# Group statistics without TensorE, the weighted sums' two halves as two tiles, and one running sum emitted later

## The chip, the core and the metric

The kernel runs on one core of a Trainium2 chip. The core has five engines that run at the same time and wait for one another through semaphores: TensorE (PE; its weight loads are shown apart, as PEld), VectorE (DVE), ScalarE (ACT), GpSimd (POOL) and SyncE (SP, which only issues DMAs here). The metric is the time of one execution in microseconds (us) of the device; the median of several runs counts, and less is better.

## What is computed

A batch of 16 images with 512 channels and 32 x 32 pixels goes through a group norm, attention over the 1024 pixels with four heads of 128 channels, and a projection, with the input added at the end. All is in 32-bit floats.

```python
xg = x.reshape(b, 8, -1)                      # 8 groups of 64 channels
mu, var = mean(xg), var(xg)
xn = ((xg - mu) * rsqrt(var + 1e-5)) * gamma + beta
q, k, v = split(qkv_w @ xn + qkv_b)           # per pixel, 3 x 512 channels
attn = softmax(q @ k.T * 128 ** -0.5)         # 4 heads, 1024 x 1024 each
out = proj_w @ (attn @ v) + proj_b
return x + out
```

## The kernel before

An image lies as four chunks of 128 channels (partitions) by 1024 pixels. The products with qkv_w and proj_w are done by Strassen's scheme in two levels (`two_levels`, `strassen`): 49 products of 128 x 128 by 256 pixels instead of 64, made by the matmuls of L604, with differences of the operands ahead of them (L572), evictions of the PSUM banks behind them (L484 and L626 on ACT, L628 on DVE) and sums of the results (L677). Its banks carry the tags x and y, two of each. The projection's last steps, L824 and L827, add bias and input on DVE and store the result.

The main loop goes through the attention steps `s`, 16 images x 4 heads x 8 blocks of 128 keys. A step works in two halves of 512 queries: `scores` makes the transposed scores of a block (L844) and their exponential on ACT (L850), `weighted_sum` of the block before adds up values by weights in PSUM (L912, the tile `po`), and at a head's last block ACT copies the result out (L919). The sum of the exponentials for the softmax is kept on DVE as a running sum `tot` over the blocks (L856, L858), and every image and head has `added[b, h, j]`, the instruction of block j's sum. Once per head `denominators` reduces `tot`, and `divide` (L922) applies the inverse.

Between these halves, the loop runs `units`: pieces of the neighbouring images' other work that `plan_head` lays into the head's eight blocks. Head 0 carries the second half of the image's q and k, head 1 the projection of the image before, head 2 the first half of the next image's q and k, head 3 the next image's v. Head 1 also has the next image's statistics: `load_x`, in blocks 2 and 3 `stats_chunk` for each chunk on ACT (two passes with an accumulator, L262 and L265, and copies that scale by 1/N, L263, L264, L268), then `stats_group`, then `normalise` (L109 on ACT, a few of image 1 on DVE by L112) in blocks 5 and 6, then the first differences of x (L317).

A group's 64 channels are half the partitions of a chunk, so the channels' means have to be averaged across partitions. `stats_group` does it by PE: a product of the 128 x 128 matrix `avg` (1/64 within each group) with the means, `pm` (L83), and one with the variances, `pv` (L88), each 4 columns wide. Around them stand small DVE instructions on 128 x 4 elements (L82, L84 to L87, L89), a power of -0.5 on POOL (L90), and scale and shift (L76, L100, L102). A product of 32-bit floats takes two PE instructions, so pm and pv are four.

The order in which an engine gets its instructions is made ahead of time by a planner. It goes by the order of emission, moves what stands under `tc.high_priority(URGENT)` ahead, takes into account when it reckons the operands to be ready, and keeps an instruction under `tc.issue_after(i)` behind `i` on that engine. Each engine then runs its instructions strictly in that order, and waits where an operand or a tile isn't free. A tile of a pool is free for its next use when all that read the last one are done.

Image 0 is a special case: its own statistics are done in an opening, and its first heads also prepare the weights' Strassen sums for v and the projection on DVE (`kept_group`, L424 to L439), store them in DRAM (L441), and load them back as needed (L406).

Of the kernel before, what the change touches and what calls it, by code (L numbers as in the profile page):

```python
# [10 lines left out]
F32 = mybir.dt.float32  # L11
I32 = mybir.dt.int32
AF = mybir.ActivationFunctionType
# [3 lines left out]
P = 128  # L17
# [169 lines left out]
def fast_path(ctx, tc, x, sources, out, consts, flag, dims):  # L187
# [33 lines left out]

    spans = one.tile([BLK, B * HEADS], F32, name="spans")
    ones = one.tile([BLK, 1], F32, name="ones")
    xs, xb, vs, qs, ks, os_, ob = {}, {}, {}, {}, {}, {}, {}
    mvs, scaled = {}, {}

# [19 lines left out]
    for g in range(P // GC):  # L246
        nc.vector.memset(avg[ts(g, GC), ts(g, GC)], 1.0 / GC)
    nc.vector.memset(neghalf, -0.5)
    for t, src in (
        (gamma_sb, gamma), (beta_sb, beta), (qkb_sb, qk_b), (vb_sb, v_b), (projb_sb, proj_b)  # L250
    ):
        nc.gpsimd.dma_start(t, src)
# [1 line left out]
    norm = Norm(nc, gn, ps_a, avg, neghalf, gamma_sb, beta_sb, NCC, N, "y")  # L254

    def stats_chunk(b, c):
        if c == 0:
            mvs[b] = gn.tile([P, NCC, 2], F32, tag="mv", name=f"mv_{b}")

        junk = lpool.tile([P, N], F32, tag="tt", name=f"junk_{b}_{c}")  # L260
        sums = gn.tile([P, 3], F32, tag="st", name=f"sums_{b}_{c}")
        nc.scalar.activation(junk, xs[b, c], AF.Identity, accum_out=sums[:, 0:1])  # L262
        nc.scalar.mul(mvs[b][:, c, 0:1], sums[:, 0:1], 1.0 / N)  # L263
        nc.scalar.mul(sums[:, 1:2], sums[:, 0:1], -1.0 / N)  # L264
        nc.scalar.activation(  # L265
            junk, xs[b, c], AF.Square, bias=sums[:, 1:2], accum_out=sums[:, 2:3]
        )
        nc.scalar.mul(mvs[b][:, c, 1:2], sums[:, 2:3], 1.0 / N)  # L268

    def stats_group(b):  # L270


        g = []

        def part(n, first, last):
            if not g:
                g.extend(norm.group_steps(mvs[b]))
            with tc.issue_after(added[b - 1, 1, n].ins), tc.high_priority(URGENT):
                for step in g[first:last]:
                    step()  # L280

        def scale():
            n = 4 if b > 1 else 3
            part(n, 9, 10)
            with tc.issue_after(added[b - 1, 1, n].ins), tc.high_priority(URGENT):
                mu, sc = norm.result
                sh = norm.shift(mu, sc)
            for c in range(NCC):
                scaled[b, c] = sc, sh, c

        return [lambda: part(2, 0, 6), lambda: part(3, 6, 9), scale]

    def normalise(b, c, half, on_scalar=True):
        t = xs[b, c][:, ts(half, HALF)]
# [171 lines left out]
    def run(units):  # L466
        for u in units:
            u()
# [372 lines left out]
    def scores(s, half):  # L841
        b, h, j = where(s)
        sc = ps_s.tile([P, HALF], F32, tag="s", name=f"s_{s}_{half}")
        nc.tensor.matmul(  # L844
            sc, ks[b, h][:, ts(j, P)], qs[b, h][:, ts(half, HALF)], start=True, stop=True
        )
        if half == 0:
            ps[s] = ppool.tile([P, N], F32, tag="p", name=f"p_{s}")
        with tc.high_priority(URGENT):
            exps[s] = nc.scalar.activation(ps[s][:, ts(half, HALF)], sc, AF.Exp, scale=SCALE)  # L850
        i = ts(half, HALF) if s == steps - 1 else ds(0, N)
        if j == 0 or (half == 0 and s < steps - 1):
            return
        if j == 1:
            tot[b, h] = lpool.tile([P, N], F32, tag="tot", name=f"tot_{b}_{h}")
            nc.vector.tensor_add(tot[b, h], ps[s - 1], ps[s])  # L856
        else:
            added[b, h, j] = nc.vector.tensor_add(  # L858
                tot[b, h][:, i], tot[b, h][:, i], ps[s][:, i]
            )  # L860
# [45 lines left out]

    def weighted_sum(s, half):
        b, h, j = where(s)
        if j == 0 and half == 0:
            po[b, h] = ps_o.tile([P, N], F32, tag="o", name=f"po_{b}_{h}")  # L910
        i = ts(half, HALF)
        nc.tensor.matmul(  # L912
            po[b, h][:, i], v_block(b, h, j), ps[s][:, i],
            start=(j == 0), stop=(j == NB - 1),
        )
        if j == NB - 1:
            if (b, h) not in os_:
                os_[b, h] = opool.tile([P, N], F32, tag="o", name=f"o_{b}_{h}")
            last_eviction[b] = nc.scalar.copy(os_[b, h][:, i], po[b, h][:, i])  # L919

    def divide(b, h):
        nc.vector.tensor_mul(os_[b, h], os_[b, h], rinv.pop((b, h)))  # L922
# [136 lines left out]
    def plan_head(b, h):  # L1059

        plan = [[] for _ in range(NB)]
        if h == 0:
            spread(plan, staggered(next_qk.pop()), 0, NB)
            if b > 0:
                plan[6].append(lambda: o_blocks(b - 1))
                plan[6].append(lambda: sums_of_b(ob[b - 1]))
            else:
                plan[5].append(lambda: stage_blocks("v"))
        elif h == 1:
            if b > 0:  # L1070
                spread(plan, staggered(proj_groups(b - 1)), 0, NB)
            if b + 1 == B:
                plan[0].append(lambda: last_loads("x"))
            else:
                plan[0].append(lambda: load_x(b + 1))
                spread(plan, [lambda c=c: stats_chunk(b + 1, c) for c in range(NCC)], 2, 4)
                sums, power, scale = stats_group(b + 1)
                if b == 0:

                    plan[4] += [sums, power, scale]  # L1080
                else:
                    plan[4].insert(0, sums)
                    plan[4].insert((len(plan[4]) + 1) // 2, power)
                    plan[5].insert(0, scale)
                for r in range(2):
                    plan[5 + r] += [

                        lambda c=c, half=half: normalise(b + 1, c, half, b > 0 or c % 2 == 1)
                        for c in range(KC * r, KC * r + KC) for half in range(NH2)
                    ]  # L1090
                plan[6].append(lambda: x_sums(b + 1, (1,)))
            if b == 0:
                for g in range(len(OUTER)):
                    plan[g // 2].append(lambda g=g: kept_group("v", g))
                    plan[NB // 2 - 1 + g].append(lambda g=g: kept_group("proj", g))
                plan[2].append(lambda: stage_blocks("proj"))
                spread(plan, [lambda o=o: bias_of_v(o) for o in range(NCC)], 3, 5)
        elif b + 1 == B:
            if h == 2:
                plan[0].append(lambda: last_loads("w"))  # L1100
                plan[2].append(last_bias)
            else:
                os_[b, h] = opool.tile([P, N], F32, tag="o", name=f"o_{b}_{h}")
                plan[3].append(lambda: o_blocks(b))
                plan[3].append(lambda: sums_of_b(ob[b], (1,)))
                plan[5].append(lambda: sums_of_b(ob[b], (2, 3), (0,)))
        elif h == 2:
            spread(plan, staggered(qk_groups(b + 1, 0)), 0, NB)

            plan[0].insert(2, lambda: x_sums(b + 1, (2,)))  # L1110
            plan[1].append(lambda: x_sums(b + 1, (3,)))
        else:

            spread(plan, staggered(next_v.pop()), 0, NB - 1)

            plan[NB - 2].append(lambda: ahead[f"qk_{b + 1}_1"]())
        return plan
# [93 lines left out]
    for s in range(steps + 1):  # L1211
        units = []
        if s < steps:
            b, h, j = where(s)
            if j == 0:
                plan = plan_head(b, h)
            units = plan[j]
            if j == NB - 1 and h == 2 and b + 1 < B:
                next_v.append(v_groups(b + 1))
                next_qk.append(qk_groups(b + 1, 1))  # L1220
                units.append(ahead[f"v_{b + 1}"])
        if NB < s < steps and s % NB == 1:
            denominators(*where(s - 2)[:2])
        for half in range(NH2):
            if s < steps:
                scores(s, half)
                if j in (1, 2) and half == 1 and s > NB:
                    with tc.issue_after(exps[s].ins):
                        spread_inverse(*where(s - NB)[:2], j - 1)
                if half == 1 and j == 4 and s > NB:  # L1230

                    with tc.issue_after(added[b, h, 4].ins):
                        divide(*where(s - NB)[:2])
            if s > 0:
                weighted_sum(s - 1, half)
            n = (len(units) + 1) // 2
            run(units[half * n : (half + 1) * n])
        if s > 0:
            del ps[s - 1]

# [135 lines left out]
```

## Time and profile before

| What | Value |
|---|---|
| median of 3 runs | 3169.19 us (3167.69 to 3172.65) |
| the profiled execution | 3171.08 us |
| its span from first to last instruction | 3169.3 us |
| granted TensorE clock | 1.0 of full speed |
| L912 and L844, weighted sums and scores on PE | 1049.4 and 1047.4 us busy |
| pm (L83) and pv (L88) on PE, 4 columns, 30 instructions each | 4.3 and 5.8 us busy |
| L858, running sums on DVE | 470.2 us busy |
| DMA | 165 GB/s over the span |

A row of the timeline has the start and the busy time in us, the engine, the line of the kernel, the operation with output and inputs, the shape, the number of instructions merged in the row, and in brackets the idle time ahead of it with what ended it. Instructions of one engine overlap in the records, since the next starts while the last one drains; the distance from start to start tells what an instruction holds its engine for. A row of the chain has start, duration, engine and line.

### The profile page before, as it was taken

To read this page: it belongs to the slowest core of one execution; us is meant where nothing else is said; L and a number is where in the kernel's file an instruction comes from. 1 tells how busy PE (TensorE), PEld (TensorE's weight loads), DVE (VectorE), ACT (ScalarE), POOL (GpSimd) and SP (SyncE) were. 2 spreads that over 40 slices of the span, in tenths; PEclk is the share of its full clock that TensorE was granted. 3 is DMA by queue.
4 is the path that set the end of the run, shared out by engine and by line. 5 is a ranking of instruction groups with operands and counts; after the bars stand their busy time and mean duration, and the time that the engine had idled before them with its cause. 6 is when DMAs were issued, how large, how long until landed. Compare 5 with 4: busy or idle time off the path is not lost.

```text
span 3169.3 us, 34227 instructions
## 1 busy us (share of the span) xinstructions
PE 3156.8 (100%) x10502; PEld 2188.2 (69%) x10502; DVE 2635.8 (83%) x4642; ACT 1438.3 (45%) x2711; POOL 516.3 (16%) x896
## 2 busy tenths in 40 slices
PE   9999999999999999999999999999999999999999
PEld 7566676677776776767767667677676776766664
DVE  9878879788897888878888787987879978788785
ACT  3535435354353443535435454453534545344333
POOL 0011221111211112211122111222012221122200
PEclk9999999999999999999999999999999999999999
DMA  5554554545545555454554545555455564555531
GB/s 176 186 190 154 187 173 152 173 152 194 168 164 163 155 184 176 167 165 144 193 173 159 170 144 192 167 174 171 144 177 170 176 187 133 178 158 187 180 119 48
DMA packets 210668, 524.83 MB, mean 166 GB/s; under 512 B 32176, under 2 KB 65456, under 8 KB 210480
## 3 DMA queue, kind: packets, MB, share of 16 engines
q1 hardware_dynamic: 133088, 282.39, 28.6%
q0 software_dynamic: 64000, 204.54, 19.3%
q10 hardware_dynamic: 13392, 35.66, 3.5%
q8 instruction: 86, 1.41, 0.2%
q14 instruction: 102, 0.84, 0.1%
HBM read 389.30 MB, written 133.17 MB: 165 GB/s over the span
## 4 chain that ended last, share of the span: by engine, by line
PE 96%; DVE 2%; DMA 1%; issue 0%; SPq 0%; POOL 0%; ACT 0%; ACTq 0%; DVEq 0%
PE s L844 27%; PE po L912 27%; PE qk_x L604 12%; PE qk_y L604 9%; PE pp_x L604 6%; PE v_x L604 6%; PE v_y L604 4%; PE pp_y L604 4%; PE lx L999 0%; DVE qk_t L572 0%; DMA x<-in_x 0%; PE ly L999 0%; DVE tot L858 0%; DVE qk_r L628 0%; DVE qk L712 0%
## 5 line engine op out<-in xcount | busy, mean ns | idle before, releaser
L912 PE MATMUL po<-p,v 128*128 128x512 f32 x2048 | 1049.4, 594 | 0.7 <-ACT p L850 0.7
L850 ACT ACTIVATE p<-s 128x512 f32<-128x512 f32 x1024 | 610.6, 596 | 963.7 <-PE s L844 960.0
L844 PE MATMUL s<-qk,qk 128*128 128x512 f32 x2048 | 1047.4, 593 | 0.3 <-DVE qk L712 0.3
L912 PEld LDWEIGHTS po<-p,v 128*128 128x128 f32 x2048 | 603.6, 302 | 322.7 <-issue 214.5
L858 DVE TENSOR_TENSOR tot<-tot,p 128x1024 f32<-128x1024 f32 x385 | 470.2, 1221 | 158.1 <-ACT p L850 156.1
L844 PEld LDWEIGHTS s<-qk,qk 128*128 128x128 f32 x2048 | 387.7, 190 | 88.6 <-issue 29.9
L604 PEld LDWEIGHTS qk_x<-qk_t,w 128*128 128x128 f32 x1344 | 251.8, 190 | 166.1 <-issue 75.3
L604 PE MATMUL qk_x<-qk_t,w 128*128 128x256 f32 x1344 | 356.3, 382 | 0.1
L484 ACT COPY qk_u<-qk_x 128x512 f32<-128x512 f32 (+1 forms) x256 | 136.2, 532 | 229.6 <-PE qk_x L604 229.6
L777 POOL DMA_DIRECT2D vd<-vu x120 | 66.6, 556 | 902.9 <-DVE vu L769 899.5
L628 DVE TENSOR_TENSOR qk_r<-qk_y,qk_u 128x512 f32<-128x512 f32 (+1 forms) x256 | 158.1, 618 | 34.7 <-ACT qk_u L484 21.5
L578 POOL DMA_DIRECT2D kept_t<-qk_t x240 | 129.3, 540 | 278.5 <-DVE qk_t L572 212.0
L604 PEld LDWEIGHTS pp_x<-pp_t,w_proj 128*128 128x128 f32 x630 | 117.2, 190 | 74.7 <-issue 32.3
L628 DVE TENSOR_TENSOR v_r<-v_y,v_u 128x512 f32<-128x512 f32 (+1 forms) x120 | 76.6, 638 | 110.5 <-ACT v_u L484 80.3
L604 PE MATMUL pp_x<-pp_t,w_proj 128*128 128x256 f32 x630 | 167.8, 383 | 0.0
L782 POOL DMA_DIRECT2D v<-vd x240 | 140.5, 592 | 166.6 <-DMA vd<-vu 63.3
L604 PE MATMUL v_x<-v_t,w_v 128*128 128x256 f32 x630 | 166.6, 381 | 0.0
L828 POOL DMA_DIRECT2D out_y<-y x120 | 65.9, 550 | 603.3 <-DVE y L827 601.5
L604 PEld LDWEIGHTS v_x<-v_t,w_v 128*128 128x128 f32 x630 | 118.4, 190 | 55.3 <-issue 19.1
L604 PE MATMUL qk_y<-x,w 128*128 128x256 f32 x512 | 142.2, 379 | 1.5 <-DVE qk_r L628 1.5
L769 DVE STREAM_TRANSPOSE vu<-vt 128x512 f32<-128x512 f32 x120 | 135.7, 1131 | 4.5 <-DMA vd<-vu 4.4
L712 DVE SCALAR_TENSOR_TENSOR qk<-qk_r,qkb_sb,qk_r 128x512 f32<-128x512 f32 x192 | 137.7, 744 | 1.6
(203 smaller groups left out, 4420.0 us busy)
## 6 DMA issues: line engine op xcount, KB each, us to landing
w<-kept SPq DMA_DIRECT2D x90, 512.0 KB, 3.7
kept_t<-qk_t POOLq DMA_DIRECT2D x180, 256.0 KB, 3.5
v_t<-kept_t SPq DMA_DIRECT2D x180, 256.0 KB, 2.9
w<-kept SPq DMA_DIRECT2D x90, 384.0 KB, 3.3
rinv<-row ACTq DMA_DIRECT2D x63, 512.0 KB, 5.0
x<-in_x POOLq DMA_DIRECT2D x60, 512.0 KB, 4.6
vd<-vu POOLq DMA_DIRECT2D x120, 256.0 KB, 3.0
v<-vd POOLq DMA_DIRECT2D x240, 128.0 KB, 4.2
```

Source lines behind the costliest of these rows:

```text
L484: nc.scalar.copy(t[n][:, :width], t["x"][:, :width])
L578: nc.gpsimd.dma_start(t, to)
L604: nc.tensor.matmul(acc[:, ts(i, Q)], have["w"][t][:, i, slot, :], inner(i, bn), start=(first and i == 0), stop=True, skip_group_check=True,)
L628: nc.vector.tensor_add(dst, view(a), view(c))
L712: nc.vector.scalar_tensor_tensor(st[b, h][:, ts(half, HALF)], a, qkb_sb[:, i : i + 1], c, ALU.add, ALU.add)
L769: nc.vector.transpose(u.rearrange("p (q i j) -> p j q i", q=n, i=BLK), t.rearrange("p (j q i) -> p j q i", q=n, i=BLK),)
L777: nc.gpsimd.dma_start(rows[which][ts(h, P), :], u)
L782: nc.gpsimd.dma_start(vs[b, pair][ts(q, BLK), half].rearrange("m h (k i) j -> m (h k) (i j)", k=n), rows[which].rearrange("(k m) (q e) -> ...
L844: nc.tensor.matmul(sc, ks[b, h][:, ts(j, P)], qs[b, h][:, ts(half, HALF)], start=True, stop=True)
L850: exps[s] = nc.scalar.activation(ps[s][:, ts(half, HALF)], sc, AF.Exp, scale=SCALE)
L858: added[b, h, j] = nc.vector.tensor_add(tot[b, h][:, i], tot[b, h][:, i], ps[s][:, i])
L912: nc.tensor.matmul(po[b, h][:, i], v_block(b, h, j), ps[s][:, i], start=(j == 0), stop=(j == NB - 1),)
```

## The change

There are three parts.

1. For images 1 to 15, the group statistics no longer use PE. ACT writes the means and the sums of squares of each chunk into columns of a tile `table` of 128 x 2 x 32, zero elsewhere, and one copy per chunk is gone. `gather` then works on DVE: it sets the counts, transposes the table in blocks of 32 x 32, so that a channel's numbers lie along a row, copies each half of a group to the other's partitions (four copies), aggregates 64 triples by one `bn_aggr`, adds epsilon, and has POOL raise one column to -0.5. `scale` transposes mean and inverse deviation back and makes scale and shift. `gather` comes behind block 3's running sum, `scale` behind block 4's (in image 0 both behind block 3's); before, there were three parts, behind blocks 2, 3 and 4.
2. The weighted sums' PSUM tile of two banks becomes two tiles of one bank, `o0` and `o1`, one for each half.
3. In head 1, block 6, of images 1 to 14, the running sum is emitted behind all other units of that block and not between its halves.

```diff
+    table = one.tile([P, 2, BLK], F32, name="table")
...
+    nc.gpsimd.memset(table, 0.0)
...
     def stats_chunk(b, c):
-        if c == 0:
-            mvs[b] = gn.tile([P, NCC, 2], F32, tag="mv", name=f"mv_{b}")
-
+        mean, spread_ = (
+            (mvs[b][:, c, 0:1], mvs[b][:, c, 1:2]) if b == 0
+            else (table[:, 0, c : c + 1], table[:, 1, c : c + 1])
+        )
...
-        nc.scalar.mul(mvs[b][:, c, 0:1], sums[:, 0:1], 1.0 / N)
+        nc.scalar.mul(mean, sums[:, 0:1], 1.0 / N)
...
-            junk, xs[b, c], AF.Square, bias=sums[:, 1:2], accum_out=sums[:, 2:3]
+            junk, xs[b, c], AF.Square, bias=sums[:, 1:2],
+            accum_out=sums[:, 2:3] if b == 0 else spread_,
         )
-        nc.scalar.mul(mvs[b][:, c, 1:2], sums[:, 2:3], 1.0 / N)
+        if b == 0:
+            nc.scalar.mul(spread_, sums[:, 2:3], 1.0 / N)
...
+        def gather():
+            t["all"] = lpool.tile([P, N], F32, tag="tt", name=f"groups_{b}")
+            rows = t["all"][:, : 6 * BLK].rearrange("p (s j) -> p s j", s=3)
+            both = t["both"] = t["all"][:, 6 * BLK : 6 * BLK + 2]
+            ve = t["all"][:, 6 * BLK + 2 : 6 * BLK + 3]
+            v.memset(rows[:, 0, :], float(N))
+            v.transpose(rows[:, 1:3, :BLK], table)
+            for q in range(quads):
+                v.tensor_copy(rows[ts(q, BLK), 1:3, BLK:], rows[ts(q ^ 1, BLK), 1:3, :BLK])
+            v.bn_aggr(both, rows.rearrange("p s j -> p j s"))
+            v.tensor_scalar_add(ve, both[:, 1:2], EPS)
+            nc.gpsimd.tensor_tensor(both[:, 1:2], ve, neghalf[:, 0:1], ALU.pow)
 
         def scale():
-            n = 4 if b > 1 else 3
-            part(n, 9, 10)
-            with tc.issue_after(added[b - 1, 1, n].ins), tc.high_priority(URGENT):
-                mu, sc = norm.result
-                sh = norm.shift(mu, sc)
+            back = t["all"][:, 8 * BLK : 10 * BLK].rearrange("p (s j) -> p s j", s=2)
+            v.transpose(back, t["both"].unsqueeze(2).to_broadcast([P, 2, BLK]))
+            sc = gn.tile([P, NCC], F32, tag="sc", name="sc")
+            v.tensor_mul(sc, back[:, 1, k], gamma_sb)
+            sh = norm.shift(back[:, 0, k], sc)
             for c in range(NCC):
                 scaled[b, c] = sc, sh, c
 
-        return [lambda: part(2, 0, 6), lambda: part(3, 6, 9), scale]
+        def part(n, step):
+            with tc.issue_after(added[b - 1, 1, n].ins), tc.high_priority(URGENT):
+                step()
+
+        return [lambda: part(3, gather), lambda: part(4 if b > 1 else 3, scale)]
...
             exps[s] = nc.scalar.activation(ps[s][:, ts(half, HALF)], sc, AF.Exp, scale=SCALE)
+        if not (h == 1 and j == 6 and 0 < b < B - 1):
+            running_sum(s, half)
+
+    def running_sum(s, half):
+        b, h, j = where(s)
         i = ts(half, HALF) if s == steps - 1 else ds(0, N)
...
-        if j == 0 and half == 0:
-            po[b, h] = ps_o.tile([P, N], F32, tag="o", name=f"po_{b}_{h}")
+        if j == 0:
+            po[half] = ps_o.tile([P, HALF], F32, tag=f"o{half}", name=f"po_{b}_{h}_{half}")
...
-                sums, power, scale = stats_group(b + 1)
+                gather, scale = stats_group(b + 1)
                 if b == 0:
-
-                    plan[4] += [sums, power, scale]
+                    plan[4] += [gather, scale]
                 else:
-                    plan[4].insert(0, sums)
-                    plan[4].insert((len(plan[4]) + 1) // 2, power)
+                    plan[4].insert(0, gather)
                     plan[5].insert(0, scale)
...
             run(units[half * n : (half + 1) * n])
+        if s < steps and h == 1 and j == 6 and 0 < b < B - 1:
+            running_sum(s, 1)
```

More of the change, by code (lines that the diff above doesn't have):

```diff
@@ L270, in stats_group @@
+        if b == 0:
+            nc.scalar.mul(spread_, sums[:, 2:3], 1.0 / N)
     def stats_group(b):
[L273 to L277, printed above, removed]
-            with tc.issue_after(added[b - 1, 1, n].ins), tc.high_priority(URGENT):
-                for step in g[first:last]:
-                    step()
-        def scale():
-            n = 4 if b > 1 else 3
-            part(n, 9, 10)
-            with tc.issue_after(added[b - 1, 1, n].ins), tc.high_priority(URGENT):
-                mu, sc = norm.result
-                sh = norm.shift(mu, sc)
+        v = nc.vector
@@ new lines, in stats_group @@
+        quads = P // BLK
+        k = slice(0, NCC)
+        t = {}
+        def gather():
[10 more added lines that the diff above has]
+            nc.gpsimd.tensor_tensor(both[:, 1:2], ve, neghalf[:, 0:1], ALU.pow)
@@ L908, in weighted_sum @@
         b, h, j = where(s)
-        if j == 0 and half == 0:
-            po[b, h] = ps_o.tile([P, N], F32, tag="o", name=f"po_{b}_{h}")
+        if j == 0:
+            po[half] = ps_o.tile([P, HALF], F32, tag=f"o{half}", name=f"po_{b}_{h}_{half}")
         i = ts(half, HALF)
         nc.tensor.matmul(
-            po[b, h][:, i], v_block(b, h, j), ps[s][:, i],
+            po[half], v_block(b, h, j), ps[s][:, i],
             start=(j == 0), stop=(j == NB - 1),
@@ L918, in weighted_sum @@
                 os_[b, h] = opool.tile([P, N], F32, tag="o", name=f"o_{b}_{h}")
-            last_eviction[b] = nc.scalar.copy(os_[b, h][:, i], po[b, h][:, i])
+            last_eviction[b] = nc.scalar.copy(os_[b, h][:, i], po[half])
     def divide(b, h):
```

## The prediction

> **What bounds the kernel now.** I read the page's busy times and its chain first, then the waits, then the timeline of one middle image on PE and on DVE, and at last the chain in image 0.
>
> ```profile
> PE 3156.8 (100%) x10502; PEld 2188.2 (69%) x10502; DVE 2635.8 (83%) x4642; ACT 1438.3 (45%) x2711; POOL 516.3 (16%) x896
> ...
> PE 96%; DVE 2%; DMA 1%; issue 0%; SPq 0%; POOL 0%; ACT 0%; ACTq 0%; DVEq 0%
> ```
>
> PE is busy all the time and carries 96% of the chain, and the list of waits names only 6 us in which PE waited. So PE's own instructions are the time, and an edit gains if it takes instructions or bubbles from PE's row, and loses if PE begins to wait. A busy share can hide bubbles, so I read starts instead. First the middle image's statistics in head 1 (columns: start, us, engine, line, what, count):
>
> ```profile
> 1094.26 1.03 PE L604 MATMUL pp_x<-pp_t,w_proj 128*128 128x256 f32 x4
> 1095.12 0.28 PE L83 MATMUL pm<-mean,avg 128*128 128x4 f32 x2
> 1095.26 1.11 PE L604 MATMUL pp_x<-ot,w_proj 128*128 128x256 f32 x4
> 1096.21 1.02 PE L844 MATMUL s<-qk,qk 128*128 128x512 f32 x2
> ...
> 1101.81 0.59 PE L604 MATMUL pp_y<-ot,w_proj 128*128 128x256 f32 x2
> 1102.33 0.39 PE L88 MATMUL pv<-vv,avg 128*128 128x4 f32 x2
> 1102.57 1.10 PE L844 MATMUL s<-qk,qk 128*128 128x512 f32 x2
> 1103.52 1.02 PE L912 MATMUL po<-p,v 128*128 128x512 f32 x2
> ```
>
> From start to start, four 256-column instructions take 0.86 us (1094.26 to 1095.12). Around the two averages the row stretches: pm itself holds 0.14 us (to 1095.26), and the next four instructions take 0.95 instead of 0.86; two pp_y ahead of pv take 0.52 instead of 0.43, pv holds 0.24, and the next two s take 0.95 instead of 0.86.
>
> **The change part by part.** *The averages leave PE.* pm costs 0.14 + 0.09 = 0.23 us, pv costs 0.09 + 0.24 + 0.09 = 0.42 us; with the unrounded starts 0.64 us per image. Images 2 to 15 lose both products: 14 x 0.64 = **8.9 us**, on the path. Nothing that PE does next is late: what follows pm and pv reads data that lay ready.
>
> The Trainium skill's page "TensorE: Matmul & The Clock Gate", section "Step-by-step: what each phase is for", speaks against this gain: weight loads are pulled ahead of running matmuls, so the next weights load while a matmul runs. By that rule the four small instructions would be nearly free; here the rows above measure 0.64 us, because a 4-column matmul is too short to cover the load behind it.
>
> *The averages of image 1* (made during image 0) sit elsewhere. PE waited 1.22 us there for the mean, but what PE gains in image 0 it gives back:
>
> ```profile
> 149.82 3.96 DMA kept_proj<-w_proj
> 153.79 5.28 DMA w<-kept
> ...
> 159.21 1.97 PE qk_x L604 x8
> ```
>
> PE stops for the weights that land 5.28 us after 153.79, and the chain behind that DMA is DVE's preparation of w_proj, which runs without idle time from 129.1 us but for 0.93 us ahead of sc (waiting for rstd). So here DVE sets the time, and its work grows. Removed: nine small instructions (mean to sh), each followed by the next 0.07 to 0.11 us after its start, 0.75 us in all, and the 0.93 us wait. Added, the gather: a 64-column memset and a 64-column transpose at 0.13 each (a DVE instruction here holds its engine for its recorded time less 0.08; L875 with 32 columns took 0.19, elementwise work adds 1.04 ns a column); four copies between groups of 32 partitions at 0.20 (L872 to L873, which also change partitions, start 0.19 to 0.20 apart); one bn_aggr over 192 numbers; one add at 0.07. bn_aggr's nearest row is L52, 12 numbers in 0.209 us, 0.059 above the 0.15 of the smallest instructions: at one number a cycle 192 cost 0.27, by that row's slope 0.94. Three results are read by the next instruction, 0.1 us each. That gives 1.8 to 2.5 us; I take 2.0, near the first slope since L49 (bn_stats, 512 columns, 0.69) runs at one column a cycle. The scale part: transpose 0.13, three small ones 0.21, three dependent steps 0.3: 0.65. The power on POOL, now one column, took 0.72 us for two columns, 1.08 for four at this place and 2.03 later on; I allow DVE a wait of 0.6, between 0 and 0.93. Sum for image 0: 2.0 + 0.65 + 0.6 - 0.75 - 0.93 = **1.6 us lost** (0.8 to 2.4). PE's own earlier time there goes into the wait for the weights.
>
> *The gather and scale in images 1 to 14.* They cost nothing if PE never waits for DVE. The cover is idle DVE time, and there is little of it:
>
> ```profile
> 1097.89 1.23 DVE L858 TENSOR_TENSOR tot<-tot,p 128x1024 f32<-128x1024 f32 x1 [0.61 <-ACT p L850]
> 1099.04 0.75 DVE L572 TENSOR_TENSOR pp_t<-ot,pp_t 128x256 f32<-128x256 f32 x2
> 1099.71 0.68 DVE L827 TENSOR_TENSOR y<-y,pp_r 128x512 f32<-128x512 f32 x1
> 1101.58 0.69 DVE L628 TENSOR_TENSOR pp_r<-pp_y,pp_p 128x512 f32<-128x512 f32 x1 [1.19 <-PE pp_y L604]
> ...
> 1120.23 0.42 DVE L628 TENSOR_TENSOR pp_r<-pp_y,pp_u 128x256 f32<-128x256 f32 x1
> ...
> 1121.17 1.22 DVE L858 TENSOR_TENSOR tot<-tot,p 128x1024 f32<-128x1024 f32 x1
> ```
>
> The gather comes behind the sum at 1097.89, so its inputs (ACT's last square ends at 1095.7) are there and it adds no wait. Between 1099 and 1103 DVE idles 1.5 us; of the gather's 2.0 some 0.5 stays over. From 1102.4 to 1131 the busy row shows 28.41 us of 28.60 for DVE: nothing absorbs there. The scale adds 0.65 less the 0.21 of sc, t and sh: 0.45. So DVE is about 0.9 us late after 1107 (0.6 to 1.5), against a PE that is 0.64 early. The power hides: the gather ends near 1101, the scale may not start before the sum at 1104.92 ends, and 2.03 us fit between. Behind the waiting power POOL queues the loads of y and the stores of out_y, which today wait at the same place for ve, at 1103.2, later than the gather ends. Behind the scale DVE queues o's division and the sums; it waits for nothing that is late. ACT loses one small copy per chunk and is 45% busy: nothing.
>
> Which PE wait is next? The last y bank of the projection: DVE ends reading it at 1120.65, PE writes it again at 1121.71, and its weights (0.19) load in between, so some 0.85 us are to spare. The first differences of the next image's q/k (done 1125.24, wanted at 1127.5) have 2.2 us. I take **no stall**, for one reason that the trace shows: DVE's order is not the order of emission. x's differences (L317, emitted last in block 6) run at 1113.11, ahead of that block's sum, and evictions (L628, marked urgent) stand between y's finishing steps (L824, L827), which no engine waits for soon. Eight finishing steps of 0.6 us lie from 1115.45 to 1121.17; added DVE work should push those back, not the evictions.
>
> *The running sum of block 6* moves behind its block's other work. In the trace it already runs at 1121.17, behind all but one eviction, so moving it gains nothing by itself. It guards the order above. Its readers are the sum at 1122.68 and, behind that, the differences with 2.2 us to spare; beyond that each us of lateness is one of PE.
>
> *Two tiles for the weighted sums.* In image 15, where no other products stand between heads, PE's second half waits for ACT's copy of the first half, and the next head for the second copy:
>
> ```profile
> 3082.80 1.02 PE L844 MATMUL s<-qk,qk 128*128 128x512 f32 x2
> 3083.66 1.23 PE L912 MATMUL po<-p,v 128*128 128x512 f32 x2
> ```
>
> The pair at 3083.66 lasts 0.21 us longer than its like; this occurs five times after 3080: **1.0 us** gained. In image 0 the same costs 0.08 four times, lost to the wait above. In the other images no such bubble shows. The memset of the table puts some tenths of a us ahead of POOL's first loads (gamma goes out at 1.3 us and is used at 10.5): nothing.
>
> **The sum.** -8.9 - 1.0 + 1.6 = -8.3 us. The profiled execution took 3171.08 us (span 3169.3, 1.8 around it), 1.9 above the median of 3169.19. It holds a PE wait of 1.49 us at 2998.9 behind one DMA of 5.4 us (median of its kind 3.0), which no other image has. So I put the sum on the median: **3160.9 us**. What a measurement here can tell from no change is about 0.2%, 6.3 us; the forecast is 0.26%.
>
> **The rivals.** *DVE's order stays and the y bank comes late.* Then 0.9 + 0.64 - 0.85 = 0.7 us of PE wait per image, 14 x 0.7 = 9.8: 3170.7 us, no change. For it: DVE without idle time from 1102 on. Against it: the finishing steps that can give way. *The same wait at its upper price, slower:* DVE 1.5 late gives 1.3 per image, 18 us: 3179. It decides from 1.04 us of wait per image, (8.3 + 6.3) / 14. Each 1.22 us sum that slips ahead of an eviction would do it too. *The small products were free anyway:* then only pm's and pv's matmul starts (28 ns apart) go, 14 x 4 x 0.028 = 1.6 us, and with +1.0 - 1.6 the time is 3168.2. The rows above speak against it. This is what the Trainium skill's rule above would give.
>
> **How the numbers follow.** The forecast (no stall, or under 0.15 us per image) has 0.57. The y bank late by 0.15 to 1.04 us has 0.24, free products 0.04: together 0.28 within 0.2%. Late by more, 0.15. The low end is 8.3 with image 0 at its lower bound and the lowest run as base: 3167.7 - 9.1 = 3158.6, less 1.6 if the DMA hiccup sits in the median too: 3157. The high end is the first rival, 3171; above it lies most of the slower case.
>
> **What would show it.** PE's count falls by 60; in head 1 four 256-column instructions keep 0.86 us throughout, and the same product of two images in a row is 195.1 us apart instead of 195.8 (pp_y's pieces of the chain at 695.92 and 891.69). Weights in image 0 land at about 160.7. DVE's row without idle reaches further, with evictions still ahead of L824 and L827. I am wrong if PE shows a bubble at pp_y's last product in head 1, or if the gather holds DVE over 2.5 us.

## The result and the profile after

| Kernel | Median of 10 runs each | Ratio, 95% interval | Its profiled execution |
|---|---|---|---|
| before | 3169.03 us (3167.6 to 3172.65) | | 3171.08 us, span 3169.3 |
| after | 3161.18 us (3159.85 to 3162.99) | 0.9975 [0.9967, 0.9984] | 3160.22 us, span 3158.5 |

The change gains 7.9 us, a quarter of a per cent (5 to 10 us by the interval); 3160.9 had been forecast. The page of the kernel after, busy times and chain:

```profile
PE 3147.1 (100%) x10442; PEld 2181.1 (69%) x10442; DVE 2655.5 (84%) x4687; ACT 1433.7 (45%) x2651; POOL 497.0 (16%) x897
...
PE 96%; DVE 2%; DMA 1%; issue 0%; SPq 0%; ACT 0%; POOL 0%; ACTq 0%; DVEq 0%; POOLq 0%
```

PE has 60 instructions less and is as much the bound as before; DVE has 19.7 us more work. The span shrank by 10.8 us, more than the medians differ, since before's profile holds a DMA hiccup. Read from the starts of the images' first scores (L844 before, L862 after): the 14 distances from image 1 on lost 8.1 us in sum, typically 195.22 instead of 195.79, or 0.57 each with the unrounded starts. Image 0 took 180.94 instead of 180.33, 0.6 more. In image 1 one more wait of before is gone, 0.24 us at a weighted sum (at 431.89). Image 15 lost 2.8: 1.0 for the bubbles and 1.65 for that hiccup. The rest, 0.1 and 0.4, lies ahead of image 0 and behind the last product.

The statistics of a middle image, on DVE, in the timeline of the kernel after:

```profile
1095.61 1.22 DVE L881 TENSOR_TENSOR tot<-tot,p 128x1024 f32<-128x1024 f32 x1 [0.83 <-ACT p L868]
1096.79 0.11 DVE L288 MEMSET groups<- 128x64 f32 x1
1096.82 0.19 DVE L289 STREAM_TRANSPOSE groups<-table 128x64 f32<-128x64 f32 x1
1096.93 0.38 DVE L590 TENSOR_TENSOR pp_t<-ot,pp_t 128x256 f32<-128x256 f32 x1
1097.33 0.78 DVE L291 COPY groups<-groups 32x64 f32<-32x64 f32 x4
1098.14 0.42 DVE L590 TENSOR_TENSOR pp_t<-ot,pp_t 128x256 f32<-128x256 f32 x1
1098.48 1.01 DVE L292 BATCH_NORM_AGGREGATE groups<-groups 128x2 f32<-128x192 f32 x1
1099.41 0.63 DVE L845 TENSOR_TENSOR y<-y,pp_r 128x512 f32<-128x512 f32 x1
1099.96 0.14 DVE L293 TENSOR_SCALAR groups<-groups 128x1 f32<-128x1 f32 x1
1100.02 0.68 DVE L646 TENSOR_TENSOR pp_r<-pp_y,pp_p 128x512 f32<-128x512 f32 x1
```

Read it from start to start. The memset holds DVE for 0.03 us, the transpose 0.11, the four copies 0.81, the aggregation 0.93 and the addition 0.06: 1.94 us. Where a step waits for its predecessor, the planner has put a piece of other work (L590, L845) in between, so no time goes into those waits. From 1095.61 to 1101.3 hardly 0.1 us of idle time is left; before, DVE idled 1.5 us between 1099 and 1103.

The place that the prediction watched, the projection's last y bank in head 1, first on DVE, then on PE:

```profile
1118.29 0.41 DVE L646 TENSOR_TENSOR pp_r<-pp_y,pp_u 128x256 f32<-128x256 f32 x1
...
1119.22 1.22 DVE L881 TENSOR_TENSOR tot<-tot,p 128x1024 f32<-128x1024 f32 x1
```

```profile
1118.21 1.04 PE L935 MATMUL po<-p,v 128*128 128x512 f32 x2
1119.09 0.59 PE L622 MATMUL pp_y<-o,w_proj 128*128 128x256 f32 x2
```

In before, PE's row of the same product was this (the eviction, at 1120.23, stands in the prediction):

```profile
1121.71 0.59 PE L604 MATMUL pp_y<-o,w_proj 128*128 128x256 f32 x2
```

After the change DVE starts to read the bank at 1118.29 and PE writes it at 1119.09, 0.80 us later; before it was 1.48. So 0.68 us of the margin are used up, and 1119.09 follows 1118.21 without a bubble. How late is DVE? Set against PE's front (the scores of head 1, block 3, at 1092.54 before and 1090.48 after, 2.06 apart), the next sum comes 0.21 us late (1104.92 and 1103.07), the shift (L102, 1108.47 and 1107.09) 0.68, the steps around it 0.34, this eviction 0.12 and the last sum 0.07 (1122.68 and 1120.69). The 0.9 us that the prediction reckoned with shows at none of these steps; the most is the shift's 0.68.

One small wait is new: in block 6 of head 1 PE loses 0.07 us per image at a pp_x, because ACT's copy of that bank (L502, 1112.96) stands behind a normalise (L109, 1112.25).

PE's starts in image 3, before and after, differ in nothing else: pm and pv are gone (0.14 and 0.24 us), the three products beside them each keep their usual slot (0.08 less each), and that one pp_x takes 0.07 more.

### The profile page after: what moved, and what is told of

Its sections match the earlier page's. It is cut to its first block, busy times and chain, and to the rows that moved or that the text cites. A ratio compares the mean times of both kernels' runs of the same rounds, so it can differ in the third digit from the quotient of the medians.

```text
span 3158.5 us, 34075 instructions
## 1 busy us (share of the span) xinstructions
PE 3147.1 (100%) x10442; PEld 2181.1 (69%) x10442; DVE 2655.5 (84%) x4687; ACT 1433.7 (45%) x2651; POOL 497.0 (16%) x897
## 4 chain that ended last, share of the span: by engine, by line
PE 96%; DVE 2%; DMA 1%; issue 0%; SPq 0%; ACT 0%; POOL 0%; ACTq 0%; DVEq 0%; POOLq 0%
PE po L935 27%; PE s L862 27%; PE qk_x L622 12%; PE qk_y L622 9%; PE pp_x L622 6%; PE v_x L622 6%; PE v_y L622 4%; PE pp_y L622 4%; PE lx L1022 0%; DVE qk_t L590 0%; DMA x<-in_x 0%; PE ly L1022 0%; SPq L373 0%; DVE qk L730 0%; DVE qk_r L646 0%
## 5 line engine op out<-in xcount | busy, mean ns | idle before, releaser
L862 PE MATMUL s<-qk,qk 128*128 128x512 f32 x2048 | 1046.3, 592 | 0.3 <-DVE qk L730 0.3
L881 DVE TENSOR_TENSOR tot<-tot,p 128x1024 f32<-128x1024 f32 x385 | 469.5, 1219 | 166.1 <-ACT p L868 166.1
L862 PEld LDWEIGHTS s<-qk,qk 128*128 128x128 f32 x2048 | 388.7, 190 | 89.8 <-issue 29.2
L502 ACT COPY qk_u<-qk_x 128x512 f32<-128x512 f32 (+1 forms) x256 | 136.2, 532 | 230.1 <-PE qk_x L622 230.1
L646 DVE TENSOR_TENSOR qk_r<-qk_y,qk_u 128x512 f32<-128x512 f32 (+1 forms) x256 | 157.7, 616 | 34.9 <-ACT qk_u L502 21.6
L646 DVE TENSOR_TENSOR v_r<-v_y,v_u 128x512 f32<-128x512 f32 (+1 forms) x120 | 76.2, 635 | 110.6 <-ACT v_u L502 80.3
L502 ACT COPY v_u<-v_x 128x512 f32<-128x512 f32 (+1 forms) x124 | 66.2, 534 | 157.2 <-PE v_x L622 130.4
```

The source lines that it names most:

```text
L502: nc.scalar.copy(t[n][:, :width], t["x"][:, :width])
L646: nc.vector.tensor_add(dst, view(a), view(c))
L862: nc.tensor.matmul(sc, ks[b, h][:, ts(j, P)], qs[b, h][:, ts(half, HALF)], start=True, stop=True)
L881: added[b, h, j] = nc.vector.tensor_add(tot[b, h][:, i], tot[b, h][:, i], ps[s][:, i])
```

## The experiments

The theory after the result: PE's four instructions are the whole gain; DVE's work fits into its idle time; and what keeps the y bank in time is not that finishing steps give way, but the third part, which keeps the running sum from standing ahead of an eviction. Rivals: the order holds by itself and the third part does nothing; small products are free and the gain comes from elsewhere; DVE has much room left. A second question came up on the way: which queue passes DVE's lateness on to PE.

| Kernel | Median (runs) | Before, same chip | Ratio, 95% interval | Images apart |
|---|---|---|---|---|
| e1: part 1 alone | 3166.19 (11) | 3168.6 | 0.9992 [0.9983, 1.0001] | 195.53 |
| e2: part 2 alone | 3167.03 (11) | 3168.6 | 0.9994 [0.9985, 1.0003] | 195.77 |
| e3: part 3 alone | 3168.78 (11) | 3168.6 | 1.0002 [0.9993, 1.0011] | 195.78 |
| e4: after without part 3 | 3165.33 (11) | 3168.6 | 0.9990 [0.9981, 0.9999] | 195.53 |
| e5: two idle products | 3182.55 (5) | 3168.76 | 1.0048 [1.0034, 1.0062] | 196.77 |
| e6: gather twice | 3200.56 (4) | 3168.76 | 1.0101 [1.0086, 1.0117] | 198.02 |
| e7: image 1 by PE | 3160.45 (8) | 3168.76 | 0.9973 [0.9962, 0.9983] | 195.22 |
| e8: one idle product | 3175.26 (10) | 3169.3 | 1.0019 [1.001, 1.0029] | 196.18 |
| e9: e6, normalise emitted later | 3206.76 (4) | 3169.3 | 1.012 [1.0103, 1.0137] | 198.27 |
| e10: after, normalise emitted later | 3168.71 (10) | 3169.3 | 0.9998 [0.9989, 1.0008] | 195.92 |
| e11: e6, normalise pinned on ACT | 3202.42 (4) | 3169.15 | 1.0107 [1.009, 1.0124] | 197.91 |
| e12: after, normalise pinned on ACT | 3160.24 (9) | 3169.15 | 0.9972 [0.9962, 0.9983] | 195.14 |

"Images apart" is the typical distance between two images' first scores in the profiled execution; 195.79 for before, 195.22 for after. It shows hundredths of a microsecond that the medians can't; the intervals of e1, e2 and e3 each contain 1, so for these the distances carry the reading.

**e1, e2, e3: each part alone.** e1 is after without the two tiles and with the running sum between the halves; e2 and e3 are before with one edit:

```diff
# e2
-        po = ps_o.tile([P, NH2, HALF], F32, tag="o")
+            po[half] = ps_o.tile([P, HALF], F32, tag=f"o{half}")
# e3
-        running_sum(s, half)
+        if not (h == 1 and j == 6 and 0 < b < B - 1):
+            running_sum(s, half)
...
+        if s < steps and h == 1 and j == 6 and 0 < b < B - 1:
+            running_sum(s, 1)
```

> Part 1 alone on the kernel before: statistics on DVE, one tile of two banks for the weighted sums, running sum of block 6 where it was. My theory after reading both traces: PE loses 0.64 us per image, but without the later running sum (part 3) DVE takes that 1.1 us sum ahead of the eviction of the last y bank in head 1, and PE waits about 0.4 us there in each of 14 images (5.6 us); image 15 keeps its five bubbles of 0.21 us. Time 3161.2 + 5.6 + 1.0 = 3167.8 us, and a PE gap of about 0.4 us ahead of the last pp_y product of head 1. Rival (the reason I wrote down: the planner lets other DVE work give way by itself): no gap, 3162.2 us. Rival (the small products were free): 3169 us or more, and images 195.8 us apart without any gap.

> Part 2 alone on the kernel before: the weighted sums' banks as two tiles. Theory: the five bubbles of 0.21 us in image 15 go, and nothing else on the path: 3169.0 - 1.0 = 3168.0 us, images still 195.8 us apart. Rival: the split is what saved PE time in every image: 3161 us and images 195.2 us apart.

> Part 3 alone on the kernel before: the running sum of block 6 of head 1 emitted behind the block's other work. Theory: the sum already stood behind that eviction, so DVE's order hardly changes and the time stays 3169.0 us (within 0.5). Rival: the sum held up PE in the kernel before too, and 1 us or more goes (14 x 0.08 = 1.1 us).

Measured: part 1 gives 0.25 us per image instead of 0.57, part 2 nothing per image, part 3 nothing. In image 15 the sum of PE's excess over its regular starts is 1.56 us in e1 and e3, and 0.54 in e2 and after: part 2 is worth its 1.0 us there. Against before the three parts alone make -2.4, -1.6 and +0.2 us, -3.8 together; all at once make -7.9. So two of the parts need each other. In e1 PE loses its time at the same place as in e4, which comes next.

**e4: the change without its third part.**

```diff
-        if not (h == 1 and j == 6 and 0 < b < B - 1):
-            running_sum(s, half)
+        running_sum(s, half)
...
-        if s < steps and h == 1 and j == 6 and 0 < b < B - 1:
-            running_sum(s, 1)
```

> The changed kernel without part 3. Theory: the sum of block 6 stands ahead of the last y bank's eviction again, PE waits about 0.4 us per image in head 1 there: 3161.2 + 14 x 0.4 = 3166.8 us, images 195.6 us apart. Rival (other work gives way by itself): 3161.2 us, images 195.2 us apart, no gap ahead of the last pp_y product.

The same place as above in e4's timeline, DVE, then PE:

```profile
1118.44 1.23 DVE L876 TENSOR_TENSOR tot<-tot,p 128x1024 f32<-128x1024 f32 x1
1119.58 0.43 DVE L646 TENSOR_TENSOR pp_r<-pp_y,pp_u 128x256 f32<-128x256 f32 x1
```

```profile
1118.98 1.04 PE L930 MATMUL po<-p,v 128*128 128x512 f32 x2
1120.06 0.70 PE L622 MATMUL pp_y<-o,w_proj 128*128 128x256 f32 x2
```

With the statistics on DVE, the planner now lays the 1.2 us sum ahead of the eviction, which starts 0.48 us and not 0.80 before the product that needs its bank. That product starts 1.08 after the pair ahead of it instead of 0.88, and its second instruction stretches by 0.10: 0.31 us per image, 14 x 0.31 = 4.3, and the medians differ by 4.15. PE's starts in image 3 of e4 and of after differ at this place alone. The third part is worth 4 us, but only beside the first.

**e5 and e8: what does a small product cost PE?** Both are after with unread products of 4 columns: e5 at the places of pm and pv, e8 at that of pm alone.

```diff
+                def idle_product(name):
+                    with tc.high_priority(URGENT):
+                        acc = ps_a.tile([P, HALF], F32, tag="y", name=name)
+                        nc.tensor.matmul(acc[:, :NCC], avg, neghalf, start=True, stop=True)
...
+                    plan[4].insert(0, lambda: idle_product("pm"))
# e5 only
+                    plan[4].insert((len(plan[4]) + 1) // 2, lambda: idle_product("pv"))
```

> The changed kernel with two products of avg and a constant 128 x 4 tile added for each of images 2 to 15 where pm and pv stood. Nobody reads their result and they wait for no DVE or ACT work of the statistics; they only take two y banks as pm and pv did. Theory: a 4-column product costs PE its own two weight loads and the cover of the next one, 0.2 us, so two cost 0.45 to 0.64 us (pv's late start, 0.09, may be missing): 3161.2 + 14 x 0.55 = 3168.9 us. Rival (small products are free, what was saved was the wait for DVE): 3161.2 + 14 x 4 x 0.028 = 3162.8 us.

> The kernel after, and in images 1 to 14, at the place of pm alone, one unread 4-column product like pm (two fp32 passes) into a y bank. In e5 the product at this place held PE for 0.28 us in its row and stretched the next products, 0.22 us in all, and it waited for no bank; the second one, at pv's place, waited for its bank. Theory (a small product costs PE its own weight loads, about 0.22 us when no bank is in the way): 14 x 0.22 = 3.1 us more than after, 3164.3 us, images 195.44 us apart. Rival (even this product's cost comes from the y bank that it takes, the bank coming free later for the projection): part or all of the other 1.33 us per image of e5 stays, up to 14 x 1.5 = 21 us, 3182 us. Rival (small products are free): 3161.2 us.

Both kernels lost far more than the products hold, and the timeline of e5 on PE and its list of waits (us in total, times, longest) say why:

```profile
1096.18 0.28 PE L1105 MATMUL pm<-neghalf,avg 128*128 128x4 f32 x2
1096.32 0.68 PE L622 MATMUL pp_y<-pp_t,w_proj 128*128 128x256 f32 x2
1096.84 1.02 PE L862 MATMUL s<-qk,qk 128*128 128x512 f32 x2
```

```profile
PE pv L1105 <- DVE pp_r L646: 8.9, 14, 0.6
```

The product itself holds PE 0.14 us, and the next pair takes 0.52 instead of 0.43: 0.22 with the unrounded starts, in e5 and in e8 alike (28 ns between its instructions, 112 and 83 behind them). That is what the prediction read from before, so small products are not free. The Trainium skill gives a weight load P / 1.2 ns for P columns ("TensorE: Matmul & The Clock Gate", section "LDWEIGHTS (loading the stationary operand)"), an estimate of 107 ns for 128. The 112 ns slot is near it, though the rows of these loads show 0.19 us each, and no run here tries another width. The rest is not PE's: pv takes a y bank and waits until DVE has evicted it (0.6 us and its followers), and in e8 the extra unit made the planner choose another order, in which a copy on ACT stands behind two normalises (PE's wait for it: 0.30 us in each of 14 images, 0.8 with what it stretches). In both kernels the power on POOL also took 1.52 us instead of 0.57 in images 2 to 15, and DVE stood 0.45 us waiting for it ahead of the scale part. Neither run prices the two products together as an undisturbed pair; e12, without them and without the 0.07 us wait, lies 0.64 us per image below before.

**e6: how much room has DVE?** After, with the gather done twice in images 2 to 15.

```diff
-            v.memset(rows[:, 0, :], float(N))
...
+            for _ in range(2 if b > 1 else 1):
+                v.memset(rows[:, 0, :], float(N))
...
+                v.bn_aggr(both, rows.rearrange("p s j -> p j s"))
```

> The changed kernel with the gather's memset, transpose, four copies and bn_aggr done twice for images 2 to 15, the same result: about 1.8 us more of DVE work per image and nothing on PE. Theory after the first four runs: the last y bank of head 1 is evicted just in time, so DVE work that no idle time absorbs becomes PE waiting; of 1.8 us some 0.5 to 1.5 remain, 14 x 1.0 = 14 us: 3175 us, with the gap ahead of the last pp_y product of head 1. Rival (the reason I wrote down: finishing steps of y give way): no gap, 3161.2 us.

It costs 2.8 us per image, 39 in all, but the wait is not at the y bank that I had watched. The list of waits, and ACT's timeline:

```profile
PE pp_x L623 <- ACT pp_u L503: 30.4, 14, 2.2
```

```profile
1120.34 0.81 ACT L109 ACTIVATE x<-x,sh,sc 128x512 f32<-128x512 f32 x1 [3.63 <-DVE sh L102]
1121.06 0.56 ACT L503 COPY pp_u<-pp_x 128x512 f32<-128x512 f32 x1
```

ACT stands 3.63 us before a normalise that waits for DVE's shift, and the copy behind it, which needs nothing from DVE, keeps a PSUM bank from PE until 1121.62. The Trainium skill has ACT and DVE as strict first-in, first-out queues ("TensorE: Matmul & The Clock Gate", section "Architectural detail: the array is 16× 32×32, not 1× 128×128"); these two rows show it. From this I formed a second theory: the price is that of the queue, and with the copy ahead of the normalise the second gather would be nearly free. The rival: DVE is simply full. Not all of the lateness is the second gather itself: the power on POOL took 1.37 us here instead of 0.57, and DVE stood 0.45 us waiting for it.

**e9 and e10: the normalise emitted one block later**, e9 on e6, e10 on after.

```diff
-                    plan[5 + r] += [
+                    plan[6 + r] += [
...
-                plan[6].append(lambda: x_sums(b + 1, (1,)))
+                plan[7].append(lambda: x_sums(b + 1, (1,)))
```

> e6 (the gather done twice) with the normalising of the next image emitted one block later (blocks 6 and 7 in place of 5 and 6) and x's first differences in block 7 in place of 6. The arithmetic of DVE is that of e6. Theory (in e6 PE waited because a normalise that itself waited for DVE's shift stood at the head of ACT's queue, with the PSUM copy behind it): with the normalise emitted behind that copy, the 2.33 and 0.39 us of wait at pp_x go, images come to 195.3 to 195.9 us apart, 3162 to 3170 us. Rival (DVE is simply too full for a second gather, whoever waits): the lateness comes back in another PE wait of the same size, 198 us apart, some 3200 us.

> The kernel after with the same later normalise as e9 and the gather done once. Theory: the one PE wait that the change left per image, 0.07 us at pp_x in block 6 behind an ACT copy that stands behind a normalise, goes; images 195.15 us apart, 14 x 0.07 = 1.0 us, 3160.2 us. Rival: the later normalise makes x's differences late for the q/k products of the next head, a new PE wait of 0.3 to 1.2 us per image, 3165 to 3178 us.

e9 decides nothing: the planner still put the first normalise ahead of that copy, PE waits the same 2.33 us there, and small waits of 0.05 to 0.1 us make a typical image 0.25 us longer than in e6. Five of its images are some 1 us longer still: when PE goes on from this wait, or up to 1.3 us later, the granted TensorE clock falls to 0.50 for 3.41 us, and rows whose starts lie 0.86 us apart elsewhere lie 1.43 and 1.71 apart (image 5, from 1123.03 on). In the profiles, that is more than half of what e9 loses against e6. Why the clock fell in these images and not in the others, nor in e6 after the same wait, no run shows. In e10 the new wait of 0.07 us did not go, and since x's differences (L335) now come later, the sum stands ahead of the last y bank's eviction again, with e4's 0.31 us and 0.38 us of waits in the next head: the whole gain was lost. A later emission is not a later place in a queue.

**e11 and e12: the normalise pinned on ACT** behind the exponential of block 5's second half, e11 on e6, e12 on after.

```diff
         sc, sh, i = scaled[b, c]
+        if b > 1:
+            with tc.issue_after(exps[((b - 1) * HEADS + 1) * NB + 5].ins):
+                return norm.apply(t, t, sc, sh, i, on_scalar)
         return norm.apply(t, t, sc, sh, i, on_scalar)
```

> e6 (the gather done twice in images 2 to 15) with one constraint more: on ACT, every normalise of the next image stands behind the exponential of block 5's second half. DVE's work is that of e6. Unlike e9, whose later emission left ACT's order as it was, this one puts the copy of pp_x (L503) and that exponential ahead of the first normalise on ACT. Theory (e6's PE wait comes from the copy that stands behind a normalise waiting for DVE's shift): the 2.33 us wait goes; a smaller one may come at the next copy, which stands behind one normalise, up to 0.5 us. Images 195.3 to 196.0 us apart, 3162 to 3172 us. Rival (DVE is too full for a second gather, whoever waits in front): the lateness shows up in another PE wait of about the same size, images about 198 us apart, some 3200 us.

> The kernel after with the same constraint on ACT as e11, the gather done once: the control for e11. In the kernel after the shift is early enough, so the constraint only moves the first normalise by some 0.7 us and the others close up behind it. Theory: within 2 us of after, 3159 to 3163 us, images 195.15 to 195.30 us apart (the 0.07 us wait at pp_x in block 6 stays or goes). Rival: the normalise, pushed together, makes later copies late by 0.2 to 0.7 us per image, 3164 to 3171 us.

Now ACT's copy does run ahead (at 1119.86, where PE is not held up), and e11's list of waits and DVE's timeline show:

```profile
PE pp_y L626 <- DVE pp_r L650: 35.0, 14, 2.5
```

```profile
1122.26 1.22 DVE L699 TENSOR_TENSOR pp_r<-pp_r,pp_r 128x1024 f32<-128x1024 f32 x1
1123.39 0.68 DVE L650 TENSOR_TENSOR pp_r<-pp_y,pp_u 128x512 f32<-128x512 f32 x1
```

The wait came back in another dress, a y bank (of block 5) that DVE evicts late. Measured from block 5's second scores, this eviction starts 3.73 us behind them (1123.39 and 1119.66) and in after 1.84 (1107.82 and 1105.98): 1.9 us late, about the size of the second gather, though 0.45 us of it is again DVE's wait for POOL. That PE waits 2.5 us for it has a second reason: the planner also changed PE's order, so that the product that needs this bank stands ahead of a pair of weighted sums and not behind it, and PE asks for the bank 0.87 us earlier than in after. With the pair ahead of it some 1.8 us would be left, an estimate from these starts. My second theory falls: ACT's queue was only the first to pass DVE's lateness on. In all three orders that ran (e6, e9, e11), DVE has room for one gather and none for two.

e12, the control, came out as foreseen: images 195.14 us apart, so the 0.07 us wait is gone under the pinned order (in which the planner also put that pp_x ahead of a pair of scores on PE). Its 3160.24 us beside the 3161.18 of after is what 14 x 0.08 = 1.1 us would give, but the intervals of the two ratios overlap, so it is not shown to be faster.

**e7: image 1's averages back on PE**, all else as after.

```diff
+                if b == 0:
+                    plan[4] += stats_group_pe(1)
```

> The changed kernel with image 1's statistics (made in image 0) by PE as before, and those of images 2 to 15 on DVE. Theory: in image 0 DVE's preparation of w_proj is on the path, so the DVE time that the gather and scale take there (1.6 us predicted, 1.3 us by the store of w_proj at 151.13 against 149.82) comes back: 3161.2 - 1.3 = 3159.9 us, and image 0 some 1 us shorter. Rival: PE's own wait for the mean (1.2 us) is on the path too, and it comes back instead: 3161.2 to 3162 us.

The chain in image 0, of after and then of e7:

```profile
151.13 3.04 DMA kept_proj<-w_proj
154.19 4.11 DMA w<-kept
...
158.44 1.53 PE qk_x L622 x6
```

```profile
148.84 3.97 DMA kept_proj<-w_proj
...
152.83 6.68 DMA w<-kept
...
159.64 1.97 PE qk_x L647 x8
```

DVE hands the weights over 2.3 us earlier than in after and 1.0 earlier than in before, yet PE goes on later, because the load took 6.68 us instead of 4.11 (5.28 in before) and the store ahead of it 3.97 instead of 3.04. Over the profiles of the kernels here image 0 takes 179.0 to 183.3 us; these DMAs scatter by microseconds, and in the longest one (e11) some 1.8 us come from 3.41 us at a granted clock of 0.50 behind the wait for the weights. The medians of e7 and after differ by 0.7 us, within their scatter. Which part of image 0's time belongs to the change can't be settled to better than about 1 us.

## Why the prediction was right, step by step

- **The averages leave PE, 8.9 us: right.** The slots on PE give the 0.64 us that was read from before, and e12 has 0.64 per image less than before; after has 0.57, as one wait of 0.07 came in, so 8.0. That wait sits in ACT's queue, for which the prediction had said "nothing".
- **Two tiles, 1.0 us: right.** 1.56 to 0.54 us of excess in image 15, in e2 and in after.
- **Image 0, 1.6 us lost: DVE's delay about right, the way into the time not shown.** DVE hands the weights over 1.3 us later than before. But they did not land at about 160.7, as foreseen: store and load together took 7.15 us instead of 9.24, and the weights were there at 158.30, 0.77 earlier than before. Image 0 got 0.6 longer all the same. On PE, the waits for the mean (1.2) and for the weights (0.6) gave way to one of 1.6 for the weights and one of 0.8 for differences that DVE makes for the q/k products (qk_t), in an order of PE's work that the planner had changed as well. The gather's 2.0 us came out as 1.94, but by two errors that cancel: "at one number a cycle 192 cost 0.27" was wrong, the aggregation holds DVE 0.93 us (0.94 was the other end of the bounds, the slope of the row of the same kind), while memset and waits cost 0.1 instead of 0.4. The wait for the power was 0.47 instead of 0.6.
- **No stall in images 1 to 14: right, for a wrong reason.** "Added DVE work should push those back, not the evictions" did not happen: the same finishing steps stand ahead of the last y bank's eviction as before, and what moved back behind them is one of x's first differences (L335, 1117.68), which still stands ahead of it. Two other things held. Behind the shift DVE was 0.07 to 0.34 us late instead of 0.9, since the idle 1.5 us was filled almost to the end. And the third part kept the sum behind the eviction; without it the planner puts it ahead (e4).
- **The third part "gains nothing by itself", "it guards the order above": right, but not priced.** The prediction named the case "each 1.22 us sum that slips ahead of an eviction" and left it among the rivals, without asking whether the third part is what excludes it. e4 gives its price, 4 us, half of the gain.
- **The rivals.** The y bank late by its order is what e4 shows, at 0.31 us per image instead of 0.7. Free small products are refuted by the 0.22 us in e5 and e8.
- **Why 3160.9 came out so near:** -8.0 instead of -8.9, -1.0 as predicted and +0.6 to +1.3 instead of +1.6 make -7.7 to -8.4, beside the -8.3 of the sum. Two terms were each some 0.3 to 1 us off in opposite directions; that they cancelled is luck. The number rested on the third part, too, which the prediction had priced at nothing and without which e4 stands 4 us higher.

## What to carry to other kernels

When work moves from a full engine to one that is 84% busy, count the idle time at that place and not over the span: here 1.94 us fitted into 1.5 us of idle time and what the old steps left free, and a second 1.94 us, with a slower power on POOL beside it, cost 2.8 us of PE. Lateness of the helping engine shows up in whichever queue stands first (an in-order copy on ACT, a bank's eviction on DVE); in e11, reordering that queue moved the wait to the next one without shrinking it. A part of a change that gains nothing alone may be what lets another part gain, so take it away from the whole, too, and not only try it alone.

## What the runs showed of the hardware that I had not expected

- The aggregation over 192 numbers took 1.01 us in its row. With L52's 0.209 us for 12 numbers that is 4.5 ns per number, where L49 takes 512 columns in 0.69 us.
- The four copies between groups of 32 partitions took 0.78 us in all and held DVE 0.81: none started before the one ahead had ended, while other DVE instructions start 0.08 before. The Trainium skill says that an instruction whose input or output starts in another quadrant than the last one's is held until all earlier ones have finished ("VectorE: DVE Perf Modes", section "Two Vector instructions with no wait between them"); these rows agree.
- The same one-column power on POOL took 0.57 us for the statistics of images 2 to 15 of after, where DVE mostly evicted a PSUM bank meanwhile (L646), and 1.43 for image 1's, where DVE's running sum (L881) ran beside it. In e5, e6, e8, e9 and e11 the planner put it beside the running sum for the other images as well, and it took 1.10 to 1.53 us, but for one image of e11 with 0.66; DVE then stood 0.45 us waiting for it. That the sum beside it is the cause was not tried by itself.
- A granted TensorE clock of 0.50 for 3.41 us shows up in e9 (five images), e10 (image 0) and e11 (image 0 and one more), besides the last microseconds of every run.
